# Two of sixteen scan states weighed with C on TensorE instead of on GpSimd

## The chip, the cores and the metric

The kernel runs on one core of a Trainium2 chip. The metric is the device time in microseconds (us) of one execution. Engines are named as in the profile: PE (TensorE), PEld (its weight loads), DVE (VectorE), ACT (ScalarE), POOL (GpSimd), SP (SyncE, which issues the DMAs). L1252 is line 1252 of the kernel before. "Before" was run three times: median 7284.69 us, 7281.98 to 7290.29.

## The reference, cut to what matters

Two residual layers act on an input of 2 images of 48 x 48 tokens with 768 channels, each after a group norm. The first is neighbourhood attention. The second is a state-space layer (in projection, causal convolution, selective scan forward and backward, gate, out projection). The change is in the selective scan of the second layer: 1536 channels d, 16 states n, 2304 tokens.

```python
A = -exp(A_log)
def step(h, inp):
    d_t, B_t, C_t, u_t = inp
    dA = exp(d_t[..., None] * A)                       # per channel and state
    h = dA * h + (d_t * u_t)[..., None] * B_t[:, None, :]
    y = einsum('bdn,bn->bd', h, C_t)                   # weigh with C, sum over the states
    return (h, y)
...
y = selective_scan(x, delta, A, B, C) + x * Dp
return y * silu(z)
```

B and C belong to a token and a state and are the same for every channel. Everything is fp32.

## The kernel before

**Tiles and loops.** Channels lie on the 128 partitions and tokens on the free axis. One image has 2304 tokens in 6 chunks of 384 (`CL`), and 1536 channels make 12 tiles. A *unit* is one channel tile over one chunk: 2 images x 2 directions x 6 chunks x 12 tiles = 288 units (`scan`, L1171). In a unit the 16 states go in 4 groups g of 4 (`SG`); inside `group(g)` (L1202) this happens:

- *fill* (`first`, L1212 to L1226): a buffer `hb` of 4 states x 386 columns takes du x B, one instruction over 4 x 384 elements, with a small copy of the old state into the edge columns. It runs on DVE, reading du from PSUM, or on POOL, reading u from SBUF. Group 0 is always DVE's; groups 1 to 3 have an alternative engine (`alt`), and the planner picks.
- *decay* (`step`, L1236): ACT writes exp(A x delta) into a PSUM pair `da`, one instruction per state; there are two such pairs.
- *scan* (`two_steps`, L1247): DVE scans two states at a time in place, `hb <- da, hb`.
- *weighing* (L1265): POOL multiplies the 4 states of `hb` by C, which a DMA has broadcast to all partitions, `bc[4 + g]`.
- *state* (L1272): ACT keeps the last column for the next chunk.
- *sum* (`add_up`, L1281): PE transposes each state in three blocks of 128 x 128 and adds the blocks in the PSUM bank `py`. This sums over the states and leaves y with tokens on the partitions. It is 12 transposes per group. After it the `hb` buffer is free; there are 7.

At a unit's start PE puts the x x Dp part into `py` (`direct`, L1297); at its end ACT copies `py` out to `yt` (L1310). In the backward direction another pair of transposes joins both directions in a bank `mm` and DVE multiplies by the gate (L1337, L1347).

**Chunks.** `chunk` (L1357) issues, one unit ahead, the DMAs of eight broadcast tiles `bc0` to `bc7` (four of B, four of C; L1368 to L1379), 128 partitions x 4 states x 384 tokens each. Each has one buffer, so a reload waits for the last use in the chunk before.

**PSUM.** The eight banks are: four for `da`, one `du`, one `py`, and two with the tag `mm`. The two `mm` banks serve everything else that PE computes beside the scan: delta of each unit (L1142), the joining of the directions, all projections (L382), and the second image's attention.

**What sets the order.** Every piece of work is added with an engine, an estimated cost, a key (the place in time, in units), what it reads and what it writes. `Order.run` (L153) is a list planner: it takes what can start first by the estimated costs, keeps track of buffers, and writes one static instruction order for each engine. Work of the scan is "main"; projections and attention of the other image are "jobs" spread over a range of keys. Where the plan leaves PE a gap over 0.8 us, `idle` (L1479) puts in transposes whose output nobody reads. Each engine then works through its own queue in order.

**Stages in time.** The first image's attention runs before the first scan, which starts at 1091 us. Then the scans of image 0 run forward and backward with in projections beside them; the attention of image 1 runs beside them (its scores in the `mm` banks from 2519 to 3968 us); then come the scans of image 1 with the remaining projections beside them.

Of the kernel before, what the change touches and what calls it, by code (L numbers as in the profile page):

```python
# [16 lines left out]
P = 128  # L17
# [22 lines left out]
CL = 384  # L40
# [3 lines left out]
SG = 4  # L44
NSG = NS // SG
# [48 lines left out]
class Order:  # L94
# [15 lines left out]
    @staticmethod  # L110
    def cells(uses):
        for x in uses:
            buf, parts = x if isinstance(x, tuple) else (x, range(x.parts))
            for p in (parts,) if isinstance(parts, int) else parts:
                yield buf, p
# [130 lines left out]
def tile_kernel(  # L246
# [3 lines left out]
    nc = tc.nc  # L250
# [5 lines left out]
    ident = const.tile([P, P], F32, tag="ident", name="ident")  # L256
# [9 lines left out]
    par = []  # L266
    for i, (conv_w, conv_b, xpT, dtT, dt_b, A_log, Dp) in enumerate((fwd, bwd)):
        q = {"dtT": dram.tile([RK + 1, DI], F32, tag=f"dtT{i}", name=f"dtT{i}")}
# [39 lines left out]
    def cols(l0, cl, k0=0, nk=1):  # L308

        c0, c1 = l0 // CW, (l0 + cl) // CW  # L310
        return [k * NCW + c for k in range(k0, k0 + nk) for c in range(c0, c1)]
# [7 lines left out]
    def sb(tag, shape, n, parts=1):  # L319
        return Buf(f"{tag}_{n}", wk, shape, tag, BUFS.get(tag, 1), parts)  # L320

    def ps(tag, n):
        return Buf(f"{tag}_{n}", psum, [P, 512], tag, BUFS.get(tag, 1))
# [5 lines left out]
    def add(eng, ns, fn, key, r=(), w=(), job=False, size=0, after=None, early=0, alt=None, due=False, opens=None):  # L329

        news = [x[0] if isinstance(x, tuple) else x for x in w]

        def issue():
            for v in news:
                if v.ap is None:
                    v.ap = v.pool.tile(v.shape, F32, tag=v.tag, name=v.name, bufs=v.bufs)
            fn()

        if eng == "PE":

            ns *= 1.04 if key < 0 else 1.05
        return order.add(eng, ns, issue, key, r, w, job, size, after, early, alt, due, opens)
# [4 lines left out]
    def act(n, pointers=0):  # L347
        return 60 + 90 * pointers + n * 0.833
# [822 lines left out]
    def scan(ch, k, x, dlj, duj, vt):  # L1171

        q, b, back, l0, cl, bc = (ch[v] for v in ("q", "b", "back", "l0", "cl", "bc"))
        at = x

        W = CL + 2
        cells = lambda a, n: a[:, : n * W].rearrange("p (j w) -> p j w", w=W)
        h, ends, leaves = slice(1, CL + 1), slice(0, W, CL + 1), 0 if back else CL + 1
        flip = (lambda a: a[:, ::-1]) if back else (lambda a: a)
        n = f"{ch['s']}_{k}"  # L1180
        c = slice(0, cl)
# [15 lines left out]
        nt = -(-cl // P)  # L1197
        tb = [slice(t * cl // nt, (t + 1) * cl // nt) for t in range(nt)]
        tp = cl // nt
        py = ps("py", n)  # L1200

        def group(g):  # L1202
            m = f"{n}_{g}"
            now = at + 0.25 * g
            hb = sb("hb", [P, SG * W], m, SG + 1)
            body = (hb, range(SG))
            of = (slice(None), k, slice(g * SG, (g + 1) * SG))
            was = zero if ch["first"] else state[of][:, :, 0:2] if back else state[of][:, :, 1:3]

            def first():  # L1212
                around = cells(hb, SG)[:, :, ends]
                if filled.eng == "POOL":
                    by, on = dus[:, ju, c], nc.gpsimd
                    on.tensor_copy(around, was)
                else:

                    by, on = du[:, c], nc.vector
                    on.scalar_tensor_tensor(  # L1220
                        around, du[:, : 2 * SG].rearrange("p (j e) -> p j e", e=2), 0.0, was, ALU.mult,
                        ALU.add,
                    )
                on.tensor_mul(  # L1224
                    cells(hb, SG)[:, :, h], by.unsqueeze(1).to_broadcast([P, SG, cl]), bc[g][:, :, c]
                )  # L1226

            on = {"DVE": dve(SG * cl) + 75, "POOL": SG * cl * 2.2 + 140}
            main, other = ("DVE", "POOL") if g in (0, 1) else ("POOL", "DVE")
            filled = add(  # L1230
                main, on[main], first, now - (0.35 if main == "POOL" else 0.1),
                [du, duj, bc[g], (state, k * NSG + g)], [hb], after=marks.get(marks["n"] - 6),
                alt=(other, on[other]) if g in (1, 2, 3) else None,
            )

            def step(j):  # L1236
                i = g * SG + j
                da = das[j // 2 % 2]
                add(
                    "ACT", act(cl, 1) + 45,  # L1240
                    lambda: nc.scalar.activation(  # L1241
                        cells(da, 2)[:, j % 2, h], dl[:, jd, c], AF.Exp, scale=q["A"][:, k, i : i + 1]
                    ),
                    now + 0.06 * j - 0.06, [dlj], [(da, j % 2)], due=True,
                )

            def two_steps(j):  # L1247
                da = das[j // 2 % 2]
                at2 = (slice(None), slice(j * W, (j + 2) * W))
                mark = add(  # L1250
                    "DVE", (4 * W + 42) / 0.96,
                    lambda: nc.vector.tensor_tensor_scan(  # L1252
                        flip(hb[at2]), flip(da[:, : 2 * W]), flip(hb[at2]), 0.0, ALU.mult, ALU.add
                    ),
                    now + 0.06 * j, [da], [(hb, (j, j + 1, SG))],
                )
                marks[marks["n"]] = mark
                marks["n"] += 1

            for j in range(0, SG, 2):  # L1260
                step(j)
                step(j + 1)
                two_steps(j)

            add(  # L1265
                "POOL", SG * cl * 2.03 + 10,
                lambda: nc.gpsimd.tensor_mul(  # L1267
                    cells(hb, SG)[:, :, h], cells(hb, SG)[:, :, h], bc[NSG + g][:, :, c]
                ),
                now + 0.25, [body, bc[NSG + g]], [body],  # L1270
            )
            if not ch["final"]:  # L1272
                add(
                    "ACT", 90,
                    lambda: nc.scalar.copy(
                        state[of][:, :, 1:2], cells(hb, SG)[:, :, leaves : leaves + 1]
                    ),
                    now + 0.3, [body, (hb, SG)], [(state, k * NSG + g)],
                )

            def add_up():  # L1281
                for j in range(SG):
                    for t in range(nt):
                        nc.tensor.matmul(  # L1284
                            py[:tp, t * P : (t + 1) * P], cells(hb, SG)[:, j, h][:, tb[t]], ident,
                            start=False,
                            stop=g == NSG - 1 and j == SG - 1 and t == nt - 1,
                            is_transpose=True, skip_group_check=True,
                        )

            add(
                "PE", SG * nt * 109 + 60, add_up, now + 0.45, [body, py], [py],
                opens=False if g == NSG - 1 else None,
            )


        def direct():  # L1297
# [59 lines left out]
    def chunk(b, back, i, at):  # L1357

        l0, cl = CHUNKS[i]
        s = f"{b}_{back}_{i}"  # L1360
        dt = sb("dt", [RK + 1, CL], s)
        src = xd[back][b]
        add(
            "SP", 400, lambda: nc.sync.dma_start(dt[:, :cl], src[: RK + 1, l0 : l0 + cl]), at - 1.4,
            [(src, cols(l0, cl))], [dt], size=RK * cl * 4,
        )
        bc = []
        for g in (0, 1, 2, NSG, 3, NSG + 1, NSG + 2, NSG + 3):  # L1368
            t = sb(f"bc{g}", [P, SG, CL], s)
            r = RK + 1 + g * SG  # L1370
            add(
                "SP", 400,
                lambda t=t, r=r: nc.sync.dma_start(
                    t[:, :, :cl], src[r : r + SG, l0 : l0 + cl].partition_broadcast(P)
                ),
                at - 1 + 0.25 * (g % NSG) + 0.3 * (g >= NSG), [(src, cols(l0, cl))], [t],
                size=P * SG * cl * 4,
            )
            bc.append((g, t))  # L1379
        bc = [t for g, t in sorted(bc, key=lambda x: x[0])]  # L1380
        ends = (0, NCH - 1)

        ys = ()
        if (b, back, i) == passes[-1]:
            parts = [sb(tag, [P, n, CL], f"y{tag}{n}", n) for tag, n in (("uz", 2 * KB), ("uz", KB), ("u", KB))]
            ys = [(y, k) for y in parts for k in range(y.parts)]
        return dict(
            q=par[back], b=b, back=back, l0=l0, cl=cl, dt=dt, bc=bc, s=s, i=i, ys=ys,
            first=i == ends[back], final=i == ends[not back],
        )  # L1390

# [15 lines left out]
        "po": ("mm",), "w": ("w",), "vw": 3, "ev": ("ev",),  # L1407
    }
    LATE = 4
    HEAD = ("bc4", "bc5", "bc6", "bc7", "bc0", "bc1")  # L1410
    A0, A1, P1 = (-56, -16), (50, 118), 118
    norms, norms0 = [], []
# [120 lines left out]
```

## Time and profile before

| what | before |
|---|---|
| median of 3 runs | 7284.69 us |
| the profiled execution's own time | 7284.3 us |
| its span, first to last instruction | 7282.5 us |
| scans on DVE (L1252) | 2304, between 1728 and 1769 ns |
| decay on ACT (L1241) | 4608, 584 ns mean |
| copies of `py` to `yt` on ACT (L1310) | 288, 474 ns mean |
| u x delta on POOL, 384 elements (L1166) | 288, 1007 ns mean |
| edge copies of a fill: DVE L1220 / POOL L1216 | 147 / 200 ns mean |
| granted PE clock, mean | 0.969 of full |

How to read it: the first two rows are whole executions, the third leaves out what lies before the first and after the last instruction. A profile page gives busy time for each engine, the chain of work that ended last, and groups of instructions with their count, busy time, mean duration and the idle time just before them. PE's busy time counts the filler of L1482 as well. The profile is of one execution, with no second core beside it.

### The profile page before, as it was taken

The numbers are of one execution on the slowest core, as the hardware profiler recorded it, in microseconds if no ns is written. First come the engines' busy times: TensorE is split into PE (matmuls) and PEld (weight loads), VectorE is DVE, ScalarE is ACT, GpSimd is POOL, SyncE is SP. The second block draws the span as 40 slices with busy tenths as digits, with TensorE's granted clock in tenths as the row PEclk, the third lists the DMA queues.
The fourth block names the chain that finished last, engine by engine and source line by source line (L and its number), as shares of the span: only waits on it lengthen the run. The fifth ranks groups of instructions, "written<-read, shape, count | busy, mean of one in ns | idle before, by whom it ended". The sixth has DMA issues, their size and how long they took to land.

```text
span 7282.5 us, 105644 instructions
## 1 busy us (share of the span) xinstructions
PE 6429.7 (88%) x38214; PEld 4891.8 (67%) x38214; DVE 6207.4 (85%) x7016; ACT 4924.7 (68%) x9948; POOL 5628.0 (77%) x2411
## 2 busy tenths in 40 slices
PE   7999988888899899899888888888888888889888
PEld 4555556666667766666666666666677887777777
DVE  1353449999888999888999999999999999999998
ACT  1232248788776787767888777778776666777764
POOL 0000009999988999869788899999999999999997
PEclk9999999999999999999999999999999999999999
DMA  6565453554556454554443542343466676555543
GB/s 180 169 198 154 138 162 102 157 151 127 153 163 189 137 158 137 157 166 135 134 144 94 157 141 91 100 133 110 132 178 188 170 204 201 181 165 170 168 147 107
DMA packets 1326322, 1101.03 MB, mean 151 GB/s; under 512 B 134168, under 2 KB 1316040, under 8 KB 1325768
## 3 DMA queue, kind: packets, MB, share of 16 engines
q1 hardware_dynamic: 1325800, 1094.27, 50.1%
q8 instruction: 303, 4.96, 0.3%
q14 instruction: 219, 1.79, 0.1%
HBM read 881.11 MB, written 213.57 MB: 150 GB/s over the span
## 4 chain that ended last, share of the span: by engine, by line
DVE 35%; PE 23%; POOL 15%; ACT 13%; issue 9%; DMA 4%; SPq 1%; DVEq 0%; POOLq 0%; ACTq 0%
DVE hb L1252 24%; POOL hb L1267 10%; POOL hb L1224 5%; DVE hb L1224 5%; PE mm_qk L382 5%; ACT da L1241 4%; DVE uz_u L931 3%; PE py L1284 3%; PE mm_v L382 2%; PE mm_ao L382 2%; PE mm_xin L382 1%; PE mm_z L382 1%; PE da L821 1%; ACT uz_u L924 1%; PE mm_out L382 1%
## 5 line engine op out<-in xcount | busy, mean ns | idle before, releaser
L1252 DVE TENSOR_TENSOR_SCAN hb<-da,hb 128x772 f32<-128x772 f32 x2304 | 3924.0, 1747 | 182.7 <-ACT da L1241 140.1
L1267 POOL TENSOR_TENSOR hb<-hb,bc 128x1536 f32<-128x1536 f32 x1152 | 3651.7, 3186 | 342.1 <-DVE hb L1252 286.0
L1241 ACT ACTIVATE da<-dlt,A 128x384 f32<-128x384 f32 x4608 | 2675.9, 584 | 1169.9 <-DVE hb L1252 1098.3
L1284 PE MATMUL py<-ident,hb 128*128 128x128 f32 x13824 | 1761.3, 281 | 263.8 <-POOL hb L1267 261.2
L1284 PEld LDWEIGHTS py<-ident,hb 128*128 128x128 f32 x13824 | 1591.2, 145 | 473.0 <-POOL hb L1267 366.7
L1224 POOL TENSOR_TENSOR hb<-u,bc 128x1536 f32<-128x1536 f32 x478 | 1651.7, 3455 | 38.6
L1224 DVE TENSOR_TENSOR hb<-du,bc 128x1536 f32<-128x1536 f32 x674 | 1184.7, 1758 | 23.0
L1166 POOL TENSOR_TENSOR u<-dlt,u 128x384 f32<-128x384 f32 x288 | 289.6, 1007 | 532.0 <-DMA bc<-xdf 412.9
L382 PE MATMUL mm_z<-xc,w_z 128*128 128x384 f32 x1728 | 609.9, 493 | 13.5 <-ACT uz_z L951 9.4
L1482 PE MATMUL py<-ident 128*128 128x128 f32 x4926 | 608.8, 278 | 0.0
L382 PE MATMUL mm_xin<-xc,w_x 128*128 128x390 f32 x1656 | 588.8, 498 | 21.3 <-DVE uz_u L931 8.5
L1482 PEld LDWEIGHTS py<-ident 128*128 128x128 f32 x4926 | 563.5, 143 | 25.2 <-issue 23.7
L382 PE MATMUL mm_out<-stage_y,w_o 128*128 128x192 f32 x3168 | 550.6, 331 | 15.2 <-DVE xr L1074 7.3
L382 PEld LDWEIGHTS mm_out<-stage_y,w_o 128*128 128x128 f32 x3168 | 522.1, 193 | 34.1 <-DVE xr L1074 9.3
L897 POOL MEMSET xc<- 128x18 f32 x4 | 0.5, 116 | 671.0 <-DMA dlt_qk<-in_w_qkv 671.0
L382 PEld LDWEIGHTS mm_xin<-xc,w_x 128*128 128x128 f32 x1656 | 309.3, 192 | 238.5 <-issue 23.4
L382 PEld LDWEIGHTS mm_z<-xc,w_z 128*128 128x128 f32 x1728 | 319.4, 192 | 220.6 <-ACT uz_z L951 16.5
L931 DVE SCALAR_TENSOR_TENSOR uz_u<-mm_xin,conv_w,uz_u 128x384 f32<-128x384 f32 x792 | 428.0, 607 | 36.0 <-ACT uz_u L924 32.8
L382 PE MATMUL mm_qk<-xc_xn,w_qk 128*128 128x384 f32 x1080 | 384.2, 501 | 11.7 <-ACT pT L828 2.9
L1300 PE MATMUL py<-ident,vt 128*128 128x128 f32 x864 | 160.4, 297 | 230.4 <-ACT yt L1310 230.1
L787 ACT ACTIVATE pr<-pr,sm 128x308 f32<-128x308 f32 x432 | 234.4, 543 | 134.7 <-DVE sm L781 134.2
L1300 PEld LDWEIGHTS py<-ident,vt 128*128 128x128 f32 x864 | 103.1, 148 | 295.0 <-ACT yt L1310 278.5
(171 smaller groups left out, 7043.4 us busy)
## 6 DMA issues: line engine op xcount, KB each, us to landing
w_o<-in_w_opT SPq DMA_DIRECT2D x264, 384.0 KB
bc<-xdf SPq DMA_DIRECT2D x96, 768.0 KB
bc<-xdb SPq DMA_DIRECT2D x96, 768.0 KB
w_x<-in_w_inT SPq DMA_DIRECT2D x144, 384.0 KB
w_z<-in_w_inT SPq DMA_DIRECT2D x144, 384.0 KB
w_qk<-in_w_qkv SPq DMA_DIRECT2D x108, 384.0 KB
u<-uf SPq DMA_DIRECT2D x48, 576.0 KB
sz<-uz_z SPq DMA_DIRECT2D x48, 576.0 KB
```

What stands on the lines that cost most here:

```text
L382: nc.tensor.matmul(acc[:m, o0 : o0 + cl], wb[:, wi, wo : wo + m], xb[:, xi, xo : xo + cl], start=c == 0, stop=c == n - 1,)
L787: nc.scalar.activation(pr[j].ap, pr[j].ap, AF.Exp, bias=sm[:, j : j + 1], scale=-1.0, accum_out=sm[:, 2 + j : 3 + j],)
L821: nc.tensor.transpose(bank(pt, 512 - P)[:nk, k * P : (k + 1) * P], pr[j][:, c0 : c0 + nk], ident,)
L931: nc.vector.scalar_tensor_tensor(u, px[:, at[j] : at[j] + cl], q["conv_w"][:, k, j : j + 1], u, ALU.mult, ALU.add,)
L1166: lambda j=j: nc.gpsimd.tensor_mul(u[:, j, c], dl[:, j, c], u[:, j, c]), at + 0.06 + 0.25 * j,
L1224: on.tensor_mul(cells(hb, SG)[:, :, h], by.unsqueeze(1).to_broadcast([P, SG, cl]), bc[g][:, :, c])
L1241: lambda: nc.scalar.activation(cells(da, 2)[:, j % 2, h], dl[:, jd, c], AF.Exp, scale=q["A"][:, k, i : i + 1]),
L1252: lambda: nc.vector.tensor_tensor_scan(flip(hb[at2]), flip(da[:, : 2 * W]), flip(hb[at2]), 0.0, ALU.mult, ALU.add),
L1267: lambda: nc.gpsimd.tensor_mul(cells(hb, SG)[:, :, h], cells(hb, SG)[:, :, h], bc[NSG + g][:, :, c]),
L1284: nc.tensor.matmul(py[:tp, t * P : (t + 1) * P], cells(hb, SG)[:, j, h][:, tb[t]], ident, start=False, stop=g == NSG - 1 and j == SG - 1 a ...
L1300: nc.tensor.matmul(py[:tp, t * P : (t + 1) * P], vt[:, tb[t]], ident, start=t == 0, stop=False, is_transpose=True, skip_group_check=True,)
L1482: nc.tensor.matmul(marks["py"][:, CL : CL + P], ident, ident, start=False, stop=False, is_transpose=True, skip_group_check=True,)
```

## The change

For group 0 (`TG`) of every unit, the first two (`TURNED`) of its four states are weighed in another way. For each of the two states:

1. `turn`: PE transposes the three 128 x 128 blocks of the state into a bank `mm`, so that tokens lie on the partitions.
2. `keep`: ACT copies the bank back over the state in `hb`.
3. `weigh`: PE multiplies each block by a 128 x 128 diagonal matrix of C and accumulates the product into `py`. There the sum over the states has been formed before by transposes alone.

POOL weighs only the other two states of group 0 (`rest`), and `add_up` transposes only those. Groups 1 to 3 are as before, 14 of 16 states in all.

In `chunk` the broadcast tile of C for group 0 (`bc4`) is loaded for two of its four states. For the other two, a DMA each fetches the row of C with tokens on the partitions (`ct`), and ACT builds three diagonals per state by scaling the rows of the identity, into the free half of `bc4`. The tile is now tracked in `SG` parts.

```diff
-            add(
-                "POOL", SG * cl * 2.03 + 10,
-                lambda: nc.gpsimd.tensor_mul(
-                    cells(hb, SG)[:, :, h], cells(hb, SG)[:, :, h], bc[NSG + g][:, :, c]
-                ),
-                now + 0.25, [body, bc[NSG + g]], [body],
-            )
+            s0 = ch["turned"] if g == TG else 0
+            cs = bc[NSG + g]
+            for j in range(s0):
+                acc = ps("mm", f"h{m}_{j}")
+
+                def turn(j=j, acc=acc):
+                    for t in range(nt):
+                        nc.tensor.transpose(
+                            acc[:, t * P : (t + 1) * P], cells(hb, SG)[:, j, h][:, tb[t]], ident
+                        )
+
+                def keep(j=j, acc=acc):
+                    nc.scalar.copy(cells(hb, SG)[:, j, h], acc[:, :cl])
+
+                def weigh(j=j):
+                    for t in range(nt):
+                        nc.tensor.matmul(
+                            py[:tp, t * P : (t + 1) * P], cs[:, j, t * P : (t + 1) * P],
+                            cells(hb, SG)[:, j, h][:, tb[t]], start=False, stop=False,
+                            skip_group_check=True,
+                        )
+
+                add("PE", nt * 109 + 60, turn, now + TK, [(hb, j)], [acc])
+                add("ACT", act(cl), keep, now + TK, [acc, (hb, j)], [(hb, j)])
+                add("PE", nt * 222 + 60, weigh, now + TK, [(hb, j), (cs, j), py], [py])
+            rest = (hb, range(s0, SG))
+            if s0 < SG:
+                add(
+                    "POOL", (SG - s0) * cl * 2.03 + 10,
+                    lambda: nc.gpsimd.tensor_mul(
+                        cells(hb, SG)[:, s0:, h], cells(hb, SG)[:, s0:, h], cs[:, s0:, c]
+                    ),
+                    now + 0.25, [rest, (cs, range(s0, SG))], [rest],
+                )
...
-                for j in range(SG):
+                for j in range(s0, SG):
...
+            if s0 < SG:
+                add(
+                    "PE", (SG - s0) * nt * 109 + 60, add_up, now + 0.45, [rest, py], [py],
+                    opens=False if g == NSG - 1 else None,
+                )
...
+            s0 = turned if g == NSG + TG else 0
+            key = at - 1 + 0.25 * (g % NSG) + 0.3 * (g >= NSG)
+            if s0 < SG:
+                add(
+                    "SP", 400,
+                    lambda t=t, r=r, s0=s0: nc.sync.dma_start(
+                        t[:, s0:, :cl], src[r + s0 : r + SG, l0 : l0 + cl].partition_broadcast(P)
+                    ),
+                    key, [(src, cols(l0, cl))], [(t, range(s0, SG))], size=P * (SG - s0) * cl * 4,
+                )
+            if s0:
+                ct = sb("ct", [P, s0, CL // P], s)
+                def fetch(ct=ct, r=r, s0=s0):
+                    with nc.allow_non_contiguous_dma(reason="once in a chunk"):
+                        for j in range(s0):
+                            nc.sync.dma_start(
+                                ct[:, j, :],
+                                src[r + j : r + j + 1, l0 : l0 + cl].rearrange("o (t p) -> p (o t)", p=P),
+                            )
+                add("SP", 400 * s0, fetch, key, [(src, cols(l0, cl))], [ct], size=P * cl * 4 // 2)
+                for j in range(s0):
+                    def diagonals(t=t, ct=ct, j=j):
+                        for i in range(cl // P):
+                            nc.scalar.mul(t[:, j, i * P : (i + 1) * P], ident, ct[:, j, i : i + 1])
+                    add("ACT", cl // P * 260, diagonals, key + 0.1, [ct], [(t, j)])
...
+    TG, TK = 0, 0.2
+    TURNED = lambda b, back, i: 2
```

More of the change, by code (lines that the diff above doesn't have):

```diff
@@ L1289, in add_up @@
                         )
[L1291 to L1294, printed above, removed]
+            if s0 < SG:
[3 more added lines that the diff above has]
+                )
         def direct():
@@ L1360, in chunk @@
         s = f"{b}_{back}_{i}"
+        turned = TURNED(b, back, i)
         dt = sb("dt", [RK + 1, CL], s)
@@ L1368, in chunk @@
         for g in (0, 1, 2, NSG, 3, NSG + 1, NSG + 2, NSG + 3):
-            t = sb(f"bc{g}", [P, SG, CL], s)
+            t = sb(f"bc{g}", [P, SG, CL], s, SG)
             r = RK + 1 + g * SG
[L1371 to L1378, printed above, removed]
+            s0 = turned if g == NSG + TG else 0
[23 more added lines that the diff above has]
+                    add("ACT", cl // P * 260, diagonals, key + 0.1, [ct], [(t, j)])
             bc.append((g, t))
@@ L1387, in chunk @@
         return dict(
-            q=par[back], b=b, back=back, l0=l0, cl=cl, dt=dt, bc=bc, s=s, i=i, ys=ys,
+            q=par[back], b=b, back=back, l0=l0, cl=cl, dt=dt, bc=bc, s=s, i=i, ys=ys, turned=turned,
             first=i == ends[back], final=i == ends[not back],
```

## The prediction

> **What bounds the kernel now.** I read the busy shares first, then the chain, then the same engines by stage, because an average over the whole span mixes an attention stage with the scan stage that the change is in.
>
> ```profile
> span 7282.5 us, 105644 instructions
> PE 6429.7 (88%) x38214; PEld 4891.8 (67%) x38214; DVE 6207.4 (85%) x7016; ACT 4924.7 (68%) x9948; POOL 5628.0 (77%) x2411
> DVE 35%; PE 23%; POOL 15%; ACT 13%; issue 9%; DMA 4%; SPq 1%; DVEq 0%; POOLq 0%; ACTq 0%
> DVE hb L1252 24%; POOL hb L1267 10%; POOL hb L1224 5%; DVE hb L1224 5%; PE mm_qk L382 5%; ACT da L1241 4%; DVE uz_u L931 3%; PE py L1284 3%; PE mm_v L382 2%; PE mm_ao L382 2%; PE mm_xin L382 1%; PE mm_z L382 1%; PE da L821 1%; ACT uz_u L924 1%; PE mm_out L382 1%
> ```
>
> The chain alternates between DVE's scan (L1252), POOL's weighing with C (L1267), and the fill (L1224), which may run on either. Next, busy time in stretches of 500 us: the columns are PE, PEld, DVE, ACT, POOL, then clock, DMA share and GB/s.
>
> ```profile
> 1600.00:2100.00 500.00, 434.44 (x2189) 312.91 (x2189) 455.30 (x422) 399.44 (x701) 466.48 (x206) 0.96 0.48 143
> 2600.00:3100.00 500.00, 457.74 (x2922) 339.34 (x2920) 467.06 (x530) 395.09 (x935) 441.40 (x187) 0.98 0.48 150
> 3100.00:3600.00 500.00, 453.72 (x2954) 339.28 (x2954) 426.41 (x529) 377.06 (x934) 401.27 (x171) 0.97 0.47 144
> 3600.00:4100.00 500.00, 439.19 (x2884) 324.18 (x2883) 466.78 (x614) 393.98 (x969) 406.90 (x174) 0.97 0.44 134
> 6100.00:6600.00 500.00, 446.13 (x2780) 366.83 (x2779) 492.21 (x398) 380.78 (x723) 481.02 (x203) 0.99 0.59 176
> ```
>
> Part of PE is filler: transposes of L1482 that the planner puts into gaps and that nobody needs. By the same stretches (PE, PEld):
>
> ```profile
> 2600.00:3100.00 500.00, 11.41 (x86) 9.60 (x86) 0.98 0.48 150
> 3600.00:4100.00 500.00, 61.39 (x458) 51.11 (x458) 0.97 0.44 134
> 6100.00:6600.00 500.00, 33.37 (x270) 31.01 (x270) 0.99 0.59 176
> ```
>
> So there are two regimes. Late (6100 to 6600) DVE is at 98% and POOL at 96%, while PE's real work is (446-33)/500 = 83% and ACT 76%: the pair DVE and POOL is the bound. Beside the second image's attention (2600 to 3100) real PE work is (458-11)/500 = 89%, and POOL is idle for 12 to 20%: POOL is not the bound there. The prices:
>
> ```profile
> L1252 DVE TENSOR_TENSOR_SCAN hb<-da,hb 128x772 f32<-128x772 f32 x2304 | 3924.0, 1747 | 182.7 <-ACT da L1241 140.1
> L1267 POOL TENSOR_TENSOR hb<-hb,bc 128x1536 f32<-128x1536 f32 x1152 | 3651.7, 3186 | 342.1 <-DVE hb L1252 286.0
> L1284 PE MATMUL py<-ident,hb 128*128 128x128 f32 x13824 | 1761.3, 281 | 263.8 <-POOL hb L1267 261.2
> L1224 POOL TENSOR_TENSOR hb<-u,bc 128x1536 f32<-128x1536 f32 x478 | 1651.7, 3455 | 38.6
> L1224 DVE TENSOR_TENSOR hb<-du,bc 128x1536 f32<-128x1536 f32 x674 | 1184.7, 1758 | 23.0
> L1482 PE MATMUL py<-ident 128*128 128x128 f32 x4926 | 608.8, 278 | 0.0
> ```
>
> ```profile
> L382 PE MATMUL mm_v<-w_v,xc_xn 128*128 128x128 f32 x1296 | 158.3, 281 | 9.6 <-ACT ev_v L631 3.6 <-ACT pT L828 2.9 <-ACT stage_oT L862 1.5
> ```
>
> Last, who waits: ACT waits long for DVE (it is ahead), DVE rarely for ACT.
>
> ```profile
> ACT da L1241 <- DVE hb L1252: 1098.3, 1351, 5.7
> POOL hb L1267 <- DVE hb L1252: 286.0, 144, 9.7
> DVE hb L1252 <- ACT da L1241: 140.1, 99, 5.8
> ```
>
> **What the Trainium skill says.** "FP8 and Floating Point Precision", section "TensorE Precision Notes", has a true FP32 product in four passes through the array. The trace shows two records where the program has one such product (648 products of 128x128 on w_v, 1296 records) and one record for a transpose; the price is taken from the records. "PSUM — Partial Sum Buffer", "The four PSUM rules": POOL cannot touch PSUM, so the turned states must come back through ACT or DVE; in the trace before no POOL row has a PSUM tile either. "GPSIMD Engine Reference", "1. Specifications": POOL shares its SBUF interfaces with DVE when DVE reads two SBUF inputs. The scan and the DVE fill read one operand from PSUM (da, du), and 2304 scans lie between 1728 and 1769 ns whatever POOL does: I expect no faster scan from a less busy POOL. "DMA: Bandwidth & Descriptors", "Rules for kernel authors": a strided last dimension becomes one descriptor per element, which is the form of the new fetch of C.
>
> **The change part by part.** A unit is one 128-channel tile over one chunk: 288 units, 8 scans each.
>
> *POOL loses* half a weighing per unit. A half weighing is between 3.186/2 = 1.59 us and, with the fixed part that 384 elements (L1166, 1007 ns) against 1536 (3186 ns) imply, 1007+384x1.89 = 1.73 us; I take 1.66. The saving is 1.52 us a unit, 438 us in all. It shortens the end only if fills move from DVE to POOL. A fill costs POOL 3.455 plus its edge copy 0.20 = 3.66 us, DVE 1.758 plus 0.147 = 1.91 us. If both engines finish together, x = 1.52/(3.66+1.91) = 0.27 fills move per unit and both gain 0.27x1.91 = 0.52 us: 150 us over 288 units at the most. By scans counted per stretch: 1100 to 2100 holds 44 units (23 us), 2100 to 4100 holds 88 (46 us), 4100 to the end 156 (81 us).
>
> *PE gains* six true products per unit; the six transposes only move from the sum to a bank "mm". One product is 158.3/648 = 0.244 us: 1.46 us a unit, 422 us in all. Filler covers part of it late; beside attention there is almost none.
>
> *ACT gains* two PSUM copies of 128x384 per unit at 0.474 us (the mean of L1310, the same form) and six diagonals per chunk. A diagonal by the nearest row, L1161 with one pointer operand (608 ns at 384 elements), less 256x0.833 and some 0.1 of overlap, is 0.29 us: 1.8 us a chunk, 43 us in all. ACT gets 1.1 us more a unit, 316 us in all; late that is 76% to about 82%.
>
> *Banks.* Only two PSUM banks "mm" exist, and the two turned states take one each for a transpose (0.49 us), the handoff and the copy: 1 us without a wait, 2 to 3 us behind ACT's queue. Beside attention, scores, probabilities, outputs and every projection use the same two. On PE, turning waits for the scan and the bank, weighing for ACT's copy; behind them queue the projections and the sum that gives a state buffer back. On ACT the copy waits for PE, and behind it queue the exponentials that the next scan needs. Both waits are new; the trace has none like them between scan and PE.
>
> *SP and DMA.* Two more issues per chunk; two rows of C as 4-byte elements. The nearest row, conv_b with 1536 such elements, took SP 1.2 to 1.4 us. Against this 384 KB less broadcast per chunk, 9 of 1101 MB. Fetched a unit ahead, hidden: nothing. If it landed late, the first unit's product would wait on PE, 24 times a few us.
>
> **The sum.** Late: half of 81, since PE goes from 83% to about 90% and ACT to 82%, in order: -40. First stage: ACT is at 80% and projections hold the banks long (one was held from 1302 to 1312 us): a quarter of 23, -6. Attention stage: relief of a POOL that is idle 12 to 20% of the time is worth nothing, and PE at 89% pays; between nothing (the lighter stretch 3600 to 4100, real PE 76%, absorbs it) and all of 1.46x67 units from 2100 to 3600 = 98. I take three quarters: +74. Diagonals at chunk ends: between nothing and 43, a fifth: +9. Sum +37. The profiled execution took 7284.3 us (span 7282.5 and 1.8 around it), 0.4 under the median of the runs, 7284.7. Forecast 7284.3+37 = 7321.
>
> **The rivals.**
> (1) Faster: the relief reaches DVE. For it: DVE at 98% late with only 6 us of waits for ACT after 6100. Then late three quarters (-61), first stage half (-12), attention a quarter of its 46 (-11) with PE's work absorbed, diagonals +9: 7209. Place: the fills of L1224. It decides once attention costs less than about 37 us, that is 0.55 us in each of 67 units. Against it: PE's 89%.
> (2) No change: price and gain cancel, 7284. For it: both are near 40 to 50 us.
> (3) Much slower: ACT becomes the bound. If a third of the 576 copies stands before an exponential that a scan awaits, that is 0.33x273 = 91 us, late gain gone, diagonals +9: 7384. Against it: ACT's 1098 us of waiting for DVE.
>
> **How the numbers follow.** Forecast (PE and banks beside attention outweigh a half-kept late gain) 0.37; faster 0.35; no change 0.11; ACT 0.17. 0.2% (15 us) is about what a measurement of this kernel tells from no change. Faster 0.35, within 0.11, slower 0.54. The bounds are 7284-150 = 7134 and 7284+98+91+43 = 7516. The range is 7195 to 7415: left out are the better part of the full balance below and full ACT cost above, about 0.1 each. The likeliest case alone: 7300 to 7365.
>
> **What would show it.** Right: the half weighing near 1.66 us; more than 478 fills on POOL, up to 478+78; DVE busy late still at 97% with more units per stretch; units slower between 2100 and 3600, with PE waiting there for bank or copy and less filler. Wrong: attention at its old pace (rival 1), or DVE's wait for the exponentials grown from 140 us to over 230 (rival 3); a POOL that is merely idler, with fills unmoved, would make the late gain nothing.

## The result

The changed kernel takes 7528.64 us (median of 4 runs, 7520.26 to 7531.65); the kernel before, on the same chip, 7283.33 us. The ratio is 1.0333, with a 95% interval of 1.0315 to 1.0351: 245 us slower, where 7321 us (+37) was forecast with a range up to 7415. First the page of the changed kernel: span and busy time of each engine.

```profile
span 7518.5 us, 110739 instructions
PE 6692.7 (89%) x40244; PEld 5137.6 (68%) x40244; DVE 6114.1 (81%) x6890; ACT 5177.3 (69%) x10668; POOL 5427.2 (72%) x2537
```

DVE has 93 us less work than before (6114.1 against 6207.4) and POOL 201 us less; the span grew by 236 us. So DVE stands idle for 329 us more: the relief arrived, and a larger wait took its place. By stretches of 500 us (PE, PEld, DVE, ACT, POOL, then clock, DMA share, GB/s):

```profile
1600.00:2100.00 500.00, 435.38 (x2284) 319.24 (x2282) 413.64 (x389) 384.43 (x684) 391.94 (x186) 0.96 0.44 133
3100.00:3600.00 500.00, 471.12 (x3112) 352.90 (x3110) 392.60 (x480) 369.45 (x905) 354.23 (x164) 1.00 0.46 140
6100.00:6600.00 500.00, 447.68 (x2954) 393.31 (x2955) 455.38 (x372) 357.13 (x713) 448.96 (x209) 0.98 0.60 174
```

Beside attention (second line) PE went from 454 to 471 us of 500. Late (third line) DVE fell from 98% to 91% and POOL from 96% to 90%. In the first stage (first line) they fell from 91 and 93% to 83 and 78%. The scans alone on DVE, after, then before:

```profile
1600.00:2100.00 500.00, 262.53 (x155) 0.96 0.44 133
6100.00:6600.00 500.00, 333.79 (x197) 0.98 0.60 174
```

```profile
1600.00:2100.00 500.00, 296.32 (x175) 0.96 0.48 143
6100.00:6600.00 500.00, 353.56 (x208) 0.99 0.59 176
```

11% fewer scans in the first stage and 5% fewer late, where I had expected more. With each scan assigned to its unit by the order of the program, the profiled execution of the changed kernel is behind by 8 us at the first scan, 121 at unit 44, 96 at unit 72, 194 at unit 132, 167 at unit 144 and 236 at the end. So the three stages of the forecast (up to unit 44, to unit 132, to the end) lost 113, 73 and 42 us. Next the groups of the changed kernel, split by shape:

```profile
L1252 DVE TENSOR_TENSOR_SCAN hb<-da,hb 128x772 f32<-128x772 f32 x2304 | 3928.9, 1748 | 257.1 <-ACT da L1241 184.0 <-POOL hb L1224 44.3 <-issue 6.3
L1296 POOL TENSOR_TENSOR hb<-hb,bc 128x768 f32<-128x768 f32 x288 | 485.5, 1686 | 115.9 <-DVE hb L1252 94.3 <-DMA bc<-xdb 7.7 <-DMA bc<-xdf 7.0
L1224 POOL TENSOR_TENSOR hb<-u,bc 128x1536 f32<-128x1536 f32 x541 | 1868.6, 3454 | 46.3 <-DMA bc<-xdf 2.5 <-DMA bc<-xdb 0.3
L1224 DVE TENSOR_TENSOR hb<-du,bc 128x1536 f32<-128x1536 f32 x611 | 1073.9, 1758 | 20.9
L1283 PE MATMUL py<-hb,bc 128*128 128x128 f32 x3456 | 504.7, 293 | 68.3 <-ACT hb L1279 68.2
L1274 PE MATMUL mm_h<-ident,hb 128*128 128x128 f32 x1728 | 293.0, 289 | 173.5 <-DVE hb L1252 36.4 <-DVE uz_u L931 29.4 <-DVE xr L1074 19.4
L1279 ACT COPY hb<-mm_h 128x384 f32<-128x384 f32 x576 | 265.0, 478 | 73.9 <-PE mm_h L1274 73.4
L1429 ACT ACTIVATE bc<-ident,ct 128x128 f32<-128x128 f32 x144 | 45.0, 388 | 2.4 <-PE py L1283 2.0 <-DMA ct<-xdf 0.3
```

The half weighing takes 1.69 us, and 63 fills moved from DVE to POOL. New is the idle column of the turning (L1274): PE waits 173 us ahead of it, partly for the scan, partly for work that empties a bank `mm` (L931 and L1074 are DVE reading a projection out of it). Then PE waits again for ACT's copy (L1283). Last, the waits of which the other end is a state buffer; the columns are total us, times, longest. Changed kernel, then the kernel before:

```profile
POOL hb L1216 <- PE py L1313: 223.9, 51, 21.4
DVE hb L1220 <- PE py L1313: 134.1, 48, 12.6
DVE hb L1252 <- ACT da L1241: 184.0, 154, 6.7
```

```profile
POOL hb L1216 <- PE py L1284: 41.0, 11, 21.2
DVE hb L1220 <- PE py L1284: 40.3, 6, 33.2
```

L1216 and L1220 are the first instruction of a fill. They wait for a sum on PE, which is what gives a buffer `hb` back: 358 us after, 81 before. These are waits of two engines together, so they are no share of the run's time. A timeline of the changed kernel in the first stage shows one such wait (start, duration, engine, line; rows left out):

```profile
1465.91 0.49 PE L1274 MATMUL mm_h<-ident,hb 128*128 128x128 f32 x3
...
1468.47 0.48 ACT L1279 COPY hb<-mm_h 128x384 f32<-128x384 f32 x1
...
1469.38 0.55 PE L1330 MATMUL py<-ident,vt 128*128 128x128 f32 x3 [1.67 <-ACT yt L1340]
...
1469.76 0.83 PE L1283 MATMUL py<-hb,bc 128*128 128x128 f32 x6
...
1471.09 0.49 PE L1274 MATMUL mm_h<-ident,hb 128*128 128x128 f32 x3
...
1473.96 2.35 PE L1537 MATMUL py<-ident 128*128 128x128 f32 x20
...
1475.33 0.48 ACT L1279 COPY hb<-mm_h 128x384 f32<-128x384 f32 x1
...
1476.14 0.83 PE L1283 MATMUL py<-hb,bc 128*128 128x128 f32 x6
...
1476.82 3.44 PE L1313 MATMUL py<-ident,hb 128*128 128x128 f32 x30
...
1477.78 0.17 DVE L1220 SCALAR_TENSOR_TENSOR hb<-du,state 128x8 f32<-128x8 f32 x1 [2.60 <-PE py L1313]
```

The scan of this pair ended at 1444.00; the first state was turned 22 us later. That alone held nothing up, since `py` was opened for this unit only at 1469.38 (L1330), just ahead of the first product. The second state decided: it was turned at 1471.09, and ACT took it up 3.8 us after its turning, because it was in a SiLU of a projection and the table load behind it. PE filled part of that time with transposes that nobody reads (L1537). Only then could PE add up the groups behind it, 30 transposes in a row that had been waiting, and DVE, idle for 2.6 us, got a buffer back.

Over all units the first of the two turnings starts 11.7 us on average after the scan (median 8.7). For 10.7 of these PE was busy with work that stood ahead in its queue, and for 1.0 idle; so this delay is largely the planned order, and how much of it comes from the two banks, which the planner counts too, the trace does not tell. A buffer lives 29.8 us from its fill to the end of its use on PE, against 23.7 before. There are seven.

### The profile page after: what moved, and what is told of

Read it like the earlier page. It is cut to its first block, busy times and chain, and to the rows that moved or that the text cites. A ratio compares the mean times of both kernels' runs of the same rounds, so it can differ in the third digit from the quotient of the medians.

```text
span 7518.5 us, 110739 instructions
## 1 busy us (share of the span) xinstructions
PE 6692.7 (89%) x40244; PEld 5137.6 (68%) x40244; DVE 6114.1 (81%) x6890; ACT 5177.3 (69%) x10668; POOL 5427.2 (72%) x2537
## 5 line engine op out<-in xcount | busy, mean ns | idle before, releaser
L1296 POOL TENSOR_TENSOR hb<-hb,bc 128x1536 f32<-128x1536 f32 (+1 forms) x1152 | 3222.0, 2810 | 596.6 <-DVE hb L1252 495.1
L1224 POOL TENSOR_TENSOR hb<-u,bc 128x1536 f32<-128x1536 f32 x541 | 1868.6, 3454 | 46.3 <-DMA bc<-xdf 2.5
L1313 PE MATMUL py<-ident,hb 128*128 128x128 f32 x12096 | 1517.5, 278 | 84.1 <-POOL hb L1296 80.9
L1313 PEld LDWEIGHTS py<-ident,hb 128*128 128x128 f32 x12096 | 1380.8, 143 | 225.2 <-POOL hb L1296 125.4
L1224 DVE TENSOR_TENSOR hb<-du,bc 128x1536 f32<-128x1536 f32 x611 | 1073.9, 1758 | 20.9
L1283 PE MATMUL py<-hb,bc 128*128 128x128 f32 x3456 | 504.7, 293 | 68.3 <-ACT hb L1279 68.2
L1283 PEld LDWEIGHTS py<-hb,bc 128*128 128x128 f32 x3456 | 458.5, 206 | 106.4 <-ACT hb L1279 86.7
L931 DVE SCALAR_TENSOR_TENSOR uz_u<-mm_xin,conv_w,uz_u 128x384 f32<-128x384 f32 x792 | 428.5, 607 | 74.1 <-ACT uz_u L924 70.5
L1274 PE MATMUL mm_h<-ident,hb 128*128 128x128 f32 x1728 | 293.0, 289 | 173.5 <-DVE hb L1252 36.4
L1537 PE MATMUL py<-ident 128*128 128x128 f32 x3500 | 432.1, 278 | 0.0
L1537 PEld LDWEIGHTS py<-ident 128*128 128x128 f32 x3500 | 399.9, 143 | 18.2 <-issue 16.0
```

Of the source, the lines that this page charges most:

```text
L931: nc.vector.scalar_tensor_tensor(u, px[:, at[j] : at[j] + cl], q["conv_w"][:, k, j : j + 1], u, ALU.mult, ALU.add,)
L1224: on.tensor_mul(cells(hb, SG)[:, :, h], by.unsqueeze(1).to_broadcast([P, SG, cl]), bc[g][:, :, c])
L1274: nc.tensor.transpose(acc[:, t * P : (t + 1) * P], cells(hb, SG)[:, j, h][:, tb[t]], ident)
L1283: nc.tensor.matmul(py[:tp, t * P : (t + 1) * P], cs[:, j, t * P : (t + 1) * P], cells(hb, SG)[:, j, h][:, tb[t]], start=False, stop=False, ...
L1296: lambda: nc.gpsimd.tensor_mul(cells(hb, SG)[:, s0:, h], cells(hb, SG)[:, s0:, h], cs[:, s0:, c]),
L1313: nc.tensor.matmul(py[:tp, t * P : (t + 1) * P], cells(hb, SG)[:, j, h][:, tb[t]], ident, start=False, stop=g == NSG - 1 and j == SG - 1 a ...
```

## The experiments

Three theories: **work** or PE (the true products take PE's time wherever they stand), **ACT** (the copies delay the exponentials), and **chain** or bank (a turned state waits for a bank, for ACT, and the unit's sums and buffers wait behind it). Times are medians; ratios are against the kernel before on the same chip, in parentheses their intervals. The first four runs share a 7291.69, the next four a 7288.20, the next four a 7286.97. A distance to the changed kernel is one of raw medians; taken through the kernels before, it can differ by up to 8 us, and each ratio's interval is about 12 us to either side.

**Products alone**, on the kernel before:

```diff
+            if g == 0:
+                for j in range(2):
+                    def more(j=j):
+                        for t in range(nt):
+                            nc.tensor.matmul(py[:tp, CL : CL + P], bc[NSG][:, j, t * P : (t + 1) * P],
+                                cells(hb, SG)[:, j, h][:, tb[t]], start=False, stop=False, ...)
+                    add("PE", nt * 222 + 60, more, now + 0.2, [(hb, j), bc[NSG], py], [py])
```

> The kernel before, with six true 128x128 products per unit added (288 x 6, the weight is a broadcast tile of C, the moving side a weighed state of group 0) into the 128 columns of py that nobody reads; nothing is removed, no bank mm is used, no ACT copy is made. The result of these products is not part of the output. Bank theory (a turned state waits long for one of two banks mm): this costs little, under 40 us. PE theory (the true products themselves push back the sums and with them the state buffers): most of the change's 245 us, at least 120 us. ACT theory: nothing, under 15 us.

7425.73 us, 1.0183 (1.0166 to 1.02): +134. A large part, and no bank is in it. Its waits show a path:

```profile
POOL hb L1216 <- PE py L1296: 125.5, 27, 20.6
DVE hb L1220 <- PE py L1296: 52.6, 26, 13.2
```

178 us of fills waiting for a sum, against 81: PE's sums come later and keep the buffers. The products stand behind POOL's weighing here, as they do not in the change.

**Transposes and copies without a bank**: the transposes go to `py[:, CL : CL + P]`, and `nc.scalar.copy(scr, cells(hb, SG)[:, j, h])` reads the state itself.

> The kernel before, with the change's transposes and copies but without a bank: per unit six more transposes of two weighed states of group 0 into the unread columns of py, and two ACT copies of 128x384 from hb to a scratch tile. Their results are not used. Bank theory: under 40 us. ACT theory: 100 us or more. PE theory: the six transposes are half of the PE work of six true products (0.73 against 1.46 us a unit), so about half of what the products cost, 60 to 100 us.

7392.47 us, 1.0141 (1.0125 to 1.0158): +101, more than the bank theory allowed, and what the ACT theory asked for. DVE's waits for the exponentials rose from 140 to 229 us:

```profile
DVE hb L1252 <- ACT da L1241: 228.8, 165, 5.7
```

**The same through a bank**: `acc = ps("mm", ...)`, transpose into `acc`, copy `scr <- acc`.

> As the run with transposes and copies, but the transposes go to a bank mm for each state and ACT copies from there to the scratch tile, so the only difference from it is the two banks per unit and the wait of ACT for PE. Results not used. Bank theory: at least 100 us slower than the run without the bank. PE theory and ACT theory: the same as the run without the bank within 20 us.

7423.5 us, 1.0186 (1.017 to 1.0202): +132. The bank adds 31 us, between the two theories. The runs differ in one thing more: ACT's copy took 0.509 us from SBUF in the run without the bank and 0.476 us from the bank here. And nothing else waits here for what is in the bank.

**POOL's relief given back**: the half weighing made twice (`for _ in range(2 if s0 else 1)`), planned at its full price.

> The changed kernel with the half weighing on POOL of group 0 made twice, so POOL gets back the 1.5 to 1.7 us per unit that the change took away (two states of sixteen are multiplied by C twice; this alters the output). If POOL and DVE still bound the changed kernel, it gets slower by 80 to 150 us. If the bound has moved to PE, the banks and the state buffers, it stays at 7529 within 25 us.

7570.06 us, 1.0389 (1.0371 to 1.0407), 41 us over the changed kernel (33 through the kernels before), between the two theories. So the relief is worth some 40 us in the kernel as it is.

**Copies alone**, as in the run with transposes and copies, without the transposes:

> The kernel before with only the two ACT copies of 128x384 per unit added (from a weighed state of group 0 to a scratch tile that nobody reads), 288 x 2 x 0.474 = 273 us of ACT. In the run with transposes and copies without a bank DVE waited 89 us longer for the exponentials, so: if its +101 us comes from the copies, this run is at least 70 us slower than before; if it comes from the six transposes on PE, it is within 30 us of before.

7336.56 us, 1.0064 (1.0049 to 1.0079): +48. DVE waits 213.9 us for the exponentials here. This is between the two theories too: about half of the +101 is the copies, and the rest, 53 us, is left for six transposes of 0.12 us.

**Products that wait for nothing**: the matmul of the products alone, on `ident, ident`, with reads and writes `[py], [py]`.

> The kernel before with six true products per unit as in the run with products alone, but of the identity with itself: they need only the open bank py, wait for no state and hold no state buffer. Results unread. If PE's occupied time is what costs, this is as slow as the products on states, +134 us within 35. If the cost is that they stand behind the weighing and hold a state buffer, this costs under 50 us.

7349.91 us, 1.0083 (1.0068 to 1.0098): +62. Between both theories: about half of the products' cost comes without any wait for a state. These products keep their place in `py` ahead of the sum of group 0, and most of the waiting for buffers is there already:

```profile
POOL hb L1216 <- PE py L1295: 105.0, 26, 13.7
DVE hb L1220 <- PE py L1295: 42.9, 21, 9.2
```

148 us, against 178 with the products on states. The other half comes with standing behind the weighing, by a way that these waits do not show.

**Half the PE price**, on the changed kernel: `weigh` transposes with `ident` instead of multiplying by `cs`.

> The changed kernel with the six true products per unit replaced by six transposes back into py, half their PE time (0.73 us a unit less); the multiplication by C of the two turned states is left out and the diagonals are built but not read. Same banks, copies, and waits. PE theory: half of what the products cost, 50 to 80 us faster than the changed kernel. If banks, copies and gating make up the loss: within 25 us of it.

7462.79 us, 1.0235 (1.022 to 1.0251): 66 us under the changed kernel, as the work theory said.

**The products behind group 2**, on the changed kernel: `weigh` is kept in a list and added ahead of the sum of group 3.

> The changed kernel with the two products per unit of turned states put in the program behind the sum of group 2 instead of ahead of the sum of group 0, so that the sums of groups 0 to 2 and their state buffers no longer wait for the bank, ACT's copy and the products; the work is the same, but the buffer of group 0 is held longer. If that order is a main link of the loss: faster by 60 us or more. If the amount of work is what costs: within 30 us of the changed kernel.

7537.82 us, 1.034 (1.0323 to 1.0357). No gain; by this test the order of the sums was no link. The trace tells why it was a poor test: from weighing to sum a state now waited 8.2 us instead of 12.7, but the buffers of group 0 lived 36.1 us instead of 29.1, and the mean of all four groups hardly moved (29.0 against 29.8). It shows one thing that speaks against a simple account by buffers: fills waited only 112 us for PE's products and sums, against 358 in the changed kernel, and the time stayed. DVE's wait for the exponentials grew instead, from 184 to 228 us.

**One turned state instead of two** (`TURNED = lambda b, back, i: 1`):

> The changed kernel with one turned state per unit instead of two, so half of every part: products, copies, banks and POOL's relief. If the costs are proportional to the work, half of the loss: +123 us against before, within 30. If one turned state already exhausts banks or state buffers, most of it (over +180). If two are past a threshold, little (under +60).

7368.97 us, 1.0108 (1.009 to 1.0126): +82, less than half, and none of the three cases foreseen. The second state costs twice the first (163 us).

**Only in the last quarter** (`2 if b and back else 0`):

> The changed kernel with states turned only in the last quarter, the backward direction of the second image (units 216 to 288), where DVE and POOL are busiest and the prediction gave its largest gain. By the unit starts of the changed kernel that quarter lost 43 us: +43 within 25 against before. If the loss there is only carried over from earlier stages (jobs that come late), the relief wins there and this is faster than before by 10 to 40 us.

7328.73 us, 1.0059 (1.0044 to 1.0074): +42, as its own quarter had lost in the changed kernel. Also where DVE and POOL were busiest, and with nothing carried over, the change loses.

**Six buffers instead of seven** (`"hb": 6`), before and after:

> The kernel before with six state buffers hb instead of seven. If buffers are what late sums on PE use up, the kernel before, whose buffers live 18 to 33 us from fill to the end of the sum, gets slower by some 40 to 120 us; if there are plenty, within 20 us of before.

> The changed kernel with six state buffers instead of seven. Its buffers live 24 to 41 us, so if late sums cost through the buffers, it loses clearly more by the missing one than the kernel before does (by 50 us or more beyond it). If buffers are no link of the loss, it loses the same within 25 us.

Before: 7304.32 us, 1.0025 (1.0015 to 1.0034), +17. After: 7586.55 us, 1.0412 (1.0395 to 1.0429), 58 us over the changed kernel. The missing buffer costs the changed kernel 41 us more; the buffers are a link, though this is under the 50 that I had asked for, and the kernel before had buffers to spare. The other side, eight buffers, was not tried.

**Both sets of parts together**, on the kernel before (products alone plus the run through a bank):

> The kernel before with the products of the run with products alone and the transposes, banks and copies of the run with a bank, together; nothing is removed, and the results are unread. If the parts add up: 134+132 = 266 us slower than before, within 30. If they hinder each other (a queue near full costs more per added us): over 310 us. If they hide in each other's waits: under 220 us.

7550.11 us against 7285.93, 1.0367 (1.035 to 1.0384): +264. They add up to within 2 us, so between these two sets a queue near full adds no cost of its own.

**Without diagonals**: `s0 = 0` in the chunk's loading, and the block with `ct`, `fetch` and `diagonals` taken out.

> The changed kernel without the diagonals and their fetch: the two DMAs of C with 4-byte elements and the six ACT multiplications per chunk are left out, all four states of C are broadcast as before, and the products read the broadcast rows in place of diagonals, which alters the output. If the diagonals at chunk ends cost what I gave them (9 us), within 20 us of the changed kernel. If they or the slow fetch stop the first unit of a chunk: faster by 24 times a few us, 50 us or more.

7523.47 us, 1.0328 (1.0313 to 1.0343), 5 us under the changed kernel: nothing that can be measured.

**The chain cut**, on the changed kernel:

```diff
-                acc = ps("mm", f"h{m}_{j}")
+                acc, scr = ps("mm", f"h{m}_{j}"), sb("scr", [P, CL], f"{m}_{j}")
...
-                def keep(j=j, acc=acc):
-                    nc.scalar.copy(cells(hb, SG)[:, j, h], acc[:, :cl])
+                def keep(scr=scr, acc=acc):
+                    nc.scalar.copy(scr[:, :cl], acc[:, :cl])
...
-                add("ACT", act(cl), keep, now + TK, [acc, (hb, j)], [(hb, j)])
+                add("ACT", act(cl), keep, now + TK, [acc], [scr])
```

> The changed kernel with ACT's copy of a turned state going to a scratch tile that nobody reads, and the products reading the state as it lies in hb, not turned (this alters the output). Transposes, banks, copies, products and diagonals are all there; only the chain bank, copy, product is cut, so the products and the sums behind them no longer wait for a free bank and for ACT. If that chain is the remaining cost of about 60 to 70 us: 7465 within 25. If the work alone costs: within 25 us of the changed kernel, 7529.

7419.17 us against 7285.57, 1.0176 (1.0159 to 1.0193): 109 us under the changed kernel, more than I had left over. All the work of the change is there; only the products don't wait for bank and ACT. The turning starts no earlier (12.7 us after the scan), so it is what stands behind it that costs.

```profile
POOL hb L1216 <- PE py L1313: 122.5, 30, 20.4
DVE hb L1220 <- PE py L1313: 49.1, 19, 8.3
DVE hb L1252 <- ACT da L1241: 203.9, 158, 6.0
```

Fills wait 172 us for a sum instead of 358, and the mean life of a buffer is 27.4 us. The wait for the exponentials stayed, since the copies did. The planner, which now foresees fewer gaps, also puts in less filler: 293 us, against 432 in the changed kernel and 609 before. No run leaves the filler out, so whether it is a part of the 109 us is not shown.

**What adds up.** Of the 245 us, the chain is 109, measured by taking it out. The other 136 are the work, and how they divide is argued, not shown. Products 134, copies 48, less 41 of relief, is 141. But with the 62 of the free products in place of 134 the sum is 69, and with the bank's 31 us, which should then be in it, since the turned states still use both banks when the chain is cut, it is 172. These prices were taken on the kernel before, where the added work stood behind POOL's weighing. The six transposes are moved and not added, and the diagonals are nothing.

## Why the prediction was wrong

The direction was right, and so were most prices. The size was wrong, by two terms.

- *POOL loses half a weighing, 1.66 us; up to 78 fills move.* Right: 1.69 us and 63 fills. The gain of the sum (-40 and -6) was also about what giving it back cost, some 40 us.
- *"PE gains six true products per unit", charged as +74 and beside attention alone.* This term was mis-sized. The price of one held: the twelve records of a unit's six products took 1.50 us in a row, against 1.46. But in the run with products alone the lag grows by 68 us up to unit 44, where I had charged PE with nothing, shrinks by 6 from there to unit 132, which holds the attention, and grows by 84 to the end: 147 in the profiled execution, +134 by the medians. The run with free products shows that PE's time costs even without a wait (+62), and standing on a state doubles it.
- *"Banks": 1 us without a wait, 2 to 3 us behind ACT's queue, nothing in the sum of its own.* This is the step that failed. I priced how long a state keeps a bank, and not what waits behind it. The turning starts 11.7 us after the scan; the product waits for it and for ACT's copy; the products stand ahead of every later sum of the unit in `py`; the buffers come back with these sums. I had written that "the sum that gives a state buffer back" queues behind, and gave it no number: 109 us.
- *First stage -6.* The largest miss by stage: +113. With the chain cut it is 61, so the chain has about half of it. I had seen that projections hold the banks long there, and only took it off the gain.
- *ACT +1.1 us a unit, hidden late.* The prices held (0.478 us a copy; the diagonals 45 us of busy time, forecast 43). But the copies alone cost 48 us. Rival 3 had a real mechanism, a scan waiting for exponentials, and charged 91 us for it, about twice this; in the changed kernel that wait is 184 us, under the 230 that was to be its sign.
- *Diagonals +9, fetch nothing.* Right: 5 us, inside the noise.
- *Late: half of the relief is kept, -40.* Wrong: from unit 132 to the end the lag grew by 42. Its relief is real (with the relief given back it grew by 100), and products, copies and chain together are larger. The last quarter alone, in its own run, is +42 too.
- *Attention +74.* The lag grew by 73 from unit 44 to 132, but that is luck. "PE at 89% pays" was the reason, and in that stretch the products alone cost nothing (-6), and all the work with the chain cut 9.

These figures by stage are each from one execution, and every run is planned anew, which moves work between stages: with six buffers the kernel before gained 67 us over units 44 to 132 and lost 63 after.

The range failed for the same reason: its upper end held ACT's cost or PE's cost beside attention, in a sum of one at a time, and no chain.

Left open: how the 136 us of work divide; by which wait the chain reaches DVE, since the run with the products behind group 2 had few waits for buffers and the same time; what the filler does; and why the second turned state costs twice the first (+82, then +163), while parts put on the kernel before simply add.

## What to carry to other kernels

A busy share of 80% on an engine that works through a queue in order is not 20% of room: ask what the engine hands back at the end of its work (here a state buffer), and who stops when it comes later. Before moving work to an emptier engine, count the handoffs as well as the work, and follow the accumulation order: in this kernel, where a unit's sums go into one bank in a fixed order, a late operand delays everything that is summed behind it. A relief on one of two engines that share a load moves only a part of its time to the end: 438 us of POOL were worth some 40.

## What was not expected of the hardware

The mean price of a product hangs on how many stand in a row. The changed kernel's timeline, one unit with its products apart and one with them together:

```profile
1476.14 0.83 PE L1283 MATMUL py<-hb,bc 128*128 128x128 f32 x6
1491.45 1.50 PE L1283 MATMUL py<-hb,bc 128*128 128x128 f32 x12
```

A product is two records, so three more products take 0.67 us, 0.22 each, and 0.16 us come once to each row. In the trace records start every 0.113 us in the products on states and every 0.112 us in the projection on w_v, so a true 128x128x128 fp32 product costs the same in both. The 0.29 us of the changed kernel (504.7/1728) and the 0.244 us of the projection (158.3/648) differ by the shorter rows. With 192 columns the kernel before starts a record every 0.163 us, 0.33 us a product: half as many columns again for nearly half as much time again. And fetching C as single elements, two DMAs of 384 elements each in a chunk (L1419), left nothing in the time that could be measured: SP spends a median of about 0.5 us on an issue, of which there are 48, and the run without them and without the diagonals is within 5 us.
